# Householder steps on 65 rows and columns, and first-layer products in halves

## The chip, the cores and the metric

One core of one Trainium2 chip runs the whole kernel: a stack of four graph layers in float32. The metric is the device time of one execution in microseconds, the median of three runs. The engines are called PE (TensorE, matmuls; PEld is its weight loads), DVE (VectorE), ACT (ScalarE), POOL (GpSimd) and SP (SyncE, which issues DMAs).

## The reference

`x` is 128 x 64 x 256 (batch, nodes, features), `adj` is one 64 x 64 matrix for all. Every layer is `x = x + layer(relu(layernorm(x)))`. The layers, cut to what matters here:

```
# layer 0: graph convolution, two linear maps with batch norms
A_hat = (A + I) scaled on both sides by deg^-1/2
x1  = einsum('nm,bmd->bnd', A_hat, h).reshape(-1, 256)
h1  = relu(batchnorm(x1 @ W1.T + b1))          # 256 -> 512, statistics over all 8192 rows
out = batchnorm(h1 @ W2.T + b2)                # 512 -> 256, statistics over all 8192 rows
# layer 1: spectral layer
L_norm = d^-1/2 (diag(deg) - A) d^-1/2
_, U = eigh(L_norm)                            # 64 x 64, all eigenvectors
out = U @ (relu(U.T @ h @ W1 + b1) @ W2 + b2)  # over the nodes
# layer 2: two graph mixings, then LSTMs over windows of 1 to 4 nodes
# layer 3: attention over 512 edges, softmax by source node
```

The eigenvectors depend only on `adj`; layer 0 does not need them, layer 1 needs them from its first block on.

## The kernel before

The tokens (batch x node) are cut into 16 blocks of 512. `X[i]` holds block i in SBUF.

**Layer 0** (`hidden0`, `hidden_block`, `features0`). For each block: ReLU of the normalised block on ACT into `z`; the mixing with `BDH` (two copies of A_hat on a diagonal) on PE, 128 columns at a time, copied back to `z` by ACT; then four output groups of `W1`, each the sum of two products of 128 x 128 weights by 512 columns, `ps<-z,w` in the profile. A group's result stays in one PSUM bank, from which DVE takes statistics (`bn_stats`) and ACT a copy. Five banks are used in turn. When all blocks are through, `features0` takes the second linear map: per block four ReLUs on ACT, then two output groups, each the sum of four such products, which ACT copies out and squares for sums. That is 256 products of 512 columns. In the trace every float32 matmul shows as two records, each with a weight load.

**The eigenvectors** (class `Fast`). `tridiagonal` brings the 64 x 64 matrix `A` to tridiagonal form in 62 Householder steps, `householder(c)` for c from 63 to 2. Every row quantity is kept on all 64 partitions at once. One step: ACT sums the squares of row `x` (`f_ja`) and takes the root (`f_h_s`); DVE takes the reciprocal (`f_h_r`), corrects the root (`f_h_t`), multiplies by a sign half (`f_NB`), updates two elements of `x`, takes a reciprocal (`f_KAP`); ACT scales `x` to `uk`; DVE takes a dot product of `uA` and `uk` (`f_junk`), makes `v`, and from `uk`, `v` and a row `z` the next row `x` in two operations. Beside this, PE makes the outer products `uk v` and `v uk` (one row each), DVE adds them to `A`, PE multiplies a broadcast unit column and a broadcast column of `A` with `A` (`zp`, `yp`), ACT copies `zp` to `z`, and DVE makes `uA` of `z` and `yp`. A DMA on SP puts `x` into row c of `V`.

After the last step, `vectors` scales the matrix, turns the reflectors into one matrix (`reflectors`), finds the eigenvalues with two chains of polynomials on DVE (`values`), the eigenvectors of the tridiagonal matrix (`twisted`), the eigenvectors `U`, and a verdict on them (`f_k_bad`). All engines read the verdict and branch on it (L1617, L1618): where it is bad, another method runs. Layer 1 follows the branch.

**The order.** `Plan` writes the order of layer 0 and of the Householder steps by hand: each step has an engine (T for PE, S for ACT, V for DVE), a figure for how long it holds the engine and one for when its result is ready. `chain` places a Householder operation; before it, `fill` puts in layer-0 steps (`beside`) that end within a slack (0.6 us on T, 0.3 on S and V) of the time at which the chain operation could start. The instructions are issued in exactly this order up to the last Householder operation; layer-0 steps that found no place come out after `vectors`, and a scheduler merges them with the eigenproblem's instructions on each engine's queue. Each engine then works through its queue in order.

Engine calls go through a helper, so nearly all instructions show line L799; groups are told apart by tile names. `f_` is the tile prefix of class `Fast`, `fps` and `fvps` are its PSUM tiles.

Of the kernel before, what the change touches and what calls it, by code (L numbers as in the profile page):

```python
# [8 lines left out]
F32 = mybir.dt.float32  # L9
# [775 lines left out]
GRID = 64  # L785

# [126 lines left out]
class Fast:  # L913
# [31 lines left out]
    def sum(self, out, a, s, b, op0, op1=ALU.mult, name="junk"):  # L945

        w = a.shape[-1]
        j = self.t(f"{name}{a.shape[0]}", a.shape[0], 64)
        self.o.stt(j[:, 0:w], a, s, b, op0, op1, acc=out)
# [3 lines left out]
    def constants(self):  # L953
# [6 lines left out]
        self.P = t("P", 64, 1)  # L960
        iota(self.P[:], [[0, 1]], 0, 1)
# [21 lines left out]
        o.ts(self.low[:], self.J[:64, :], self.P[:], ALU.is_lt)  # L983
# [3 lines left out]
        o.copy(pi[:], self.P[:])  # L987
# [15 lines left out]
    def tridiagonal(self, S, made, plan):  # L1003
# [3 lines left out]
        A = self.A = t("A", 64, 64)  # L1007
        m = t("SR", 64, 64)
        NB, OA, KAP, V = t("NB", 64, 64), t("OA", 64, 64, 2), t("KAP", 64, 64), t("V", 64, 64)
        nc.vector.memset(OA[:], 1.0)  # L1010
        for x in (KAP, NB, V):
            nc.vector.memset(x[:], 0.0)
        s0, r, tt, q, c2 = (t("h_" + x, 64, 1) for x in "s0 r t q c2".split())
        ja = t("ja", 64, 64)
        bc = lambda c, n=64: c.to_broadcast([n, 64])
# [5 lines left out]

        d = go("T", lambda: keep("p", S, self.JR[:]), [made], 0.3, 0.5)
        d = go("V", lambda: o.copy(m[:], now["p"][:]), [d], 0.15, 0.28)
        d = go("T", lambda: keep("p", self.JR[:], m[:]), [d], 0.3, 0.5)
        rest = go("V", lambda: o.copy(A[:], now["p"][:]), [d], 0.15, 0.28)
        d = go("T", lambda: keep("p", bc(ident[:64, 63:64]), A[:]), [rest], 0.3, 0.5)

        def first():
            x = now["x"] = self.rows.tile([64, 65], F32, name="f_x", bufs=8)
            o.copy(x[:, 0:63], now["p"][:, 0:63])  # L1030

        def square(w):
            x = now["x"]
            self.act(ja[:, 0:w], x[:, 0:w], AF.Square, accum_out=x[:, w:w + 1])

        row = go("V", first, [d], 0.15, 0.28)
        h = go("S", lambda: square(63), [row], 0.34, 0.42)
        for c in range(63, 1, -1):
            row, h, rest = self.householder(c, now, go, row, h, rest, (s0, r, tt, q, c2), square)

    def householder(self, c, now, go, row, h, rest, scalars, square):

        o, nc, t = self.o, self.nc, self.t
        ident = self.k.ident
        A, NB, OA, KAP, V = self.A, t("NB", 64, 64), t("OA", 64, 64, 2), t("KAP", 64, 64), t("V", 64, 64)
        s0, r, tt, q, c2 = scalars
        bc = lambda a, n=64: a.to_broadcast([n, 64])
        x = lambda a, b: now["x"][:, a:b]
        nb = NB[:, c - 1:c]
        e, w = 0.001 * c, c - 1  # L1050

        def zy():
            now["zp"] = self.ps.tile([64, 64], F32, name="fps")
            nc.tensor.matmul(now["zp"][:, 0:c], bc(ident[0:c, c - 1:c], c), A[0:c, 0:c], start=True, stop=True)
            now["yp"] = self.ps.tile([64, 64], F32, name="fps")
            nc.tensor.matmul(now["yp"][:, 0:c], bc(A[0:c, c:c + 1], c), A[0:c, 0:c], start=True, stop=True)

        def row_z():
            now["z"] = self.rows.tile([64, 64], F32, name="f_z")
            self.act(now["z"][:, 0:c], now["zp"][:, 0:c], AF.Copy)  # L1060

        def row_uk():

            nc.sync.dma_start(V[c:c + 1, 0:c], now["x"][0:1, 0:c])
            now["uk"] = self.rows.tile([64, 64], F32, name="f_uk")
            self.act(now["uk"][:, 0:c], x(0, c), AF.Copy, scale=KAP[:, c:c + 1])

        def row_uA():
            now["uA"] = self.rows.tile([64, 64], F32, name="f_uA")
            o.stt(now["uA"][:, 0:c], now["z"][:, 0:c], nb, now["yp"][:, 0:c], ALU.mult, ALU.add)  # L1070

        def row_v():
            now["v"] = self.rows.tile([64, 64], F32, name="f_v")
            o.stt(now["v"][:, 0:c], x(0, c), c2[:], now["uA"][:, 0:c], ALU.mult, ALU.subtract)

        def outer():
            uk, v = now["uk"], now["v"]
            p = now["p"] = self.ps.tile([64, 64], F32, name="fps")
            nc.tensor.matmul(p[0:c, 0:c], uk[0:1, 0:c], v[0:1, 0:c], start=True, stop=False)
            nc.tensor.matmul(p[0:c, 0:c], v[0:1, 0:c], uk[0:1, 0:c], start=False, stop=True)  # L1080

        def row_x():
            now["x"] = self.rows.tile([64, 65], F32, name="f_x", bufs=8)
            o.stt(x(0, w), now["uk"][:, 0:w], now["v"][:, w:c], now["z"][:, 0:w], ALU.mult, ALU.add)


        z = go("T", zy, [rest], 0.34, 0.42)
        sq = go("S", lambda: self.act(s0[:], x(c, c + 1), AF.Sqrt), [h], 0.13, 0.23)
        oa = go("S", lambda: self.act(OA[:, c, 1:2], x(c - 1, c), AF.Copy), [row], 0.12, 0.22)
        zs = go("S", row_z, [z], 0.15, 0.26 + e)  # L1090
        sg = go("V", lambda: o.ts(q[:], x(c - 1, c), **halve(0)), [row])
        d = go("V", lambda: o.recip(r[:], s0[:]), [sq])
        d = go("V", lambda: o.stt(tt[:], r[:], x(c, c + 1), s0[:], ALU.mult, ALU.add), [d, h])
        b = go("V", lambda: o.mul(nb, q[:], tt[:]), [d, sg])
        d = go("V", lambda: o.stt(x(c - 1, c + 1), OA[:, c, :], nb, x(c - 1, c + 1), ALU.mult, ALU.add), [b, oa])
        d = go("V", lambda: o.recip(KAP[:, c:c + 1], x(c, c + 1)), [d])
        uk = go("S", row_uk, [d], 0.16, 0.32 + e)
        d = go("V", row_uA, [zs, b, z], 0.12 + e, 0.25 + e)
        d = go("V", lambda: self.sum(c2[:], now["uA"][:, 0:c], 0.5, now["uk"][:, 0:c], ALU.mult), [uk, d],
               0.2 + e, 0.28 + e)  # L1100
        v = go("V", row_v, [d], 0.15 + e, 0.26 + e)
        p = go("T", outer, [v], 0.25, 0.45)
        if c > 2:
            row = go("V", row_x, [v], 0.15 + e, 0.22 + e)
            row = go("V", lambda: o.stt(x(0, w), now["v"][:, 0:w], now["uk"][:, w:c], x(0, w), ALU.mult, ALU.add),
                     [row], 0.15 + e, 0.25 + e)
            h = go("S", lambda: square(w), [row], 0.28 + e, 0.36 + e)
        rest = go("V", lambda: o.add(A[0:c, 0:c], A[0:c, 0:c], now["p"][0:c, 0:c]), [p], 0.12 + e, 0.22 + e)
        return row, h, rest

    def reflectors(self):
# [8 lines left out]
        self.sum(kc[:], self.KAPs[:], 1.0, ident, ALU.mult)  # L1120
# [22 lines left out]
    def scale(self):  # L1143

        o, nc, t = self.o, self.nc, self.t
        NB, A = t("NB", 64, 64), self.A
        self.KAPs = t("KAP", 64, 64)
        DM, NE = t("DM", 64, 64), t("NE", 64, 64)
        o.mul(DM[:], A[:], self.k.ident[:64, :64])
        pe = self.mm((self.k.ident[:64, 1:2].to_broadcast([64, 64]), A[:]))  # L1150
# [223 lines left out]
    def verdict(self, U):  # L1374
# [32 lines left out]
        NB, OA = t("NB", 64, 64), t("OA", 64, 64, 2)  # L1407
# [36 lines left out]
P = 128  # L1444
# [1342 lines left out]
```

## Time and profile before

| what | us |
|---|---|
| median of 3 runs (2323.7 to 2329.91) | 2329.01 |
| span of the profiled execution | 2325.1 |
| first and last root of the Householder steps (`f_h_s`) | 12.1 and 268.3 |
| last 512-wide layer-0 product | 363.8 |
| verdict on the eigenvectors on PE (`f_k_bad`) | 364.35 |
| last 128-wide product after the branch, layer 1's start | from 370.16 |

The profiled execution's own time is its span, 2325.1 us, which lies inside the range of the runs; the median is 3.9 above it.

A group of the profile reads: line, engine, operation, output <- inputs by tile names, partitions x elements, how often, then busy time and mean duration in ns, then idle time of the engine ahead of it and what ended it. In the time-ordered view a row is start, duration, engine, line, operation, tiles, partitions x columns of the weights and elements, count, and in brackets the idle time of the engine before it. Rows are merged where one follows another, so a row's count matters. Ends of matmuls are modelled, so their durations overlap; distances between starts tell more.

### The profile page before, as it was taken

To read this page: it belongs to the slowest core of one execution; us is meant where nothing else is said; L and a number is where in the kernel's file an instruction comes from. 1 tells how busy PE (TensorE), PEld (TensorE's weight loads), DVE (VectorE), ACT (ScalarE), POOL (GpSimd) and SP (SyncE) were. 2 spreads that over 40 slices of the span, in tenths; PEclk is the share of its full clock that TensorE was granted. 3 is DMA by queue.
4 is the path that set the end of the run, shared out by engine and by line. 5 is a ranking of instruction groups with operands and counts; after the bars stand their busy time and mean duration, and the time that the engine had idled before them with its cause. 6 is when DMAs were issued, how large, how long until landed. Compare 5 with 4: busy or idle time off the path is not lost.

```text
span 2325.1 us, 32725 instructions
## 1 busy us (share of the span) xinstructions
PE 2283.6 (98%) x12169; PEld 1633.1 (70%) x12169; DVE 1629.3 (70%) x4054; ACT 1139.5 (49%) x2483; POOL 3.0 (0%) x26
## 2 busy tenths in 40 slices
PE   7999998999999999999999999999999999999999
PEld 4554445676777788888999998888885544554544
DVE  8887676888447777666767676559756686766667
ACT  5765865754436654433444444336435544444321
POOL 0000000000000000000000000000000000000000
PEclk9999999999999999999999999999999999999999
DMA  5000211230000000001000002000010000000001
GB/s 171 1 1 26 65 56 30 71 83 19 1 37 0 1 19 1 1 1 37 1 1 1 1 1 73 1 1 17 1 46 28 1 5 15 15 19 14 14 24 46
DMA packets 61065, 54.81 MB, mean 24 GB/s; under 512 B 15203, under 2 KB 58724, under 8 KB 60900
## 3 DMA queue, kind: packets, MB, share of 16 engines
q1 hardware_dynamic: 60900, 52.66, 7.4%
q8 instruction: 97, 1.59, 0.3%
q14 instruction: 68, 0.56, 0.1%
HBM read 35.86 MB, written 16.78 MB: 23 GB/s over the span
## 4 chain that ended last, share of the span: by engine, by line
PE 79%; DVE 3%; issue 1%; ACT 1%; DMA 0%; SPq 0%; ACTq 0%; DVEq 0%
PE ps L799 69%; PE acc L799 5%; PE pt L799 4%; PE pe L799 1%; PE y L799 1%; DVE aw L799 1%; DVE X L799 1%; DVE sm_m L799 0%; DVE XV L799 0%; ACT ls_g L799 0%; ACT h L799 0%; DVE ls_g L799 0%; ACT big L799 0%; DVE ls_t L799 0%; DVE sm_e L799 0%
## 5 line engine op out<-in xcount | busy, mean ns | idle before, releaser
L799 ACT ACTIVATE ls_g<-ls_g,ls_b 128x512 f32<-128x512 f32 (+4 forms) x472 | 243.1, 565 | 151.4 <-DVE ls_g L799 149.6
L799 ACT ACTIVATE ls_g<-ps,ls_b 128x256 f32<-128x256 f32 (+3 forms) x268 | 115.5, 470 | 330.9 <-PE ps L799 327.7
L799 PE MATMUL ps<-z,w 128*128 128x512 f32 x512 | 254.9, 621 | 0.9 <-ACT z L799 0.9
L799 PE MATMUL ps<-big,X 128*128 128x176 f32 (+3 forms) x848 | 212.7, 366 | 0.1
L799 DVE TENSOR_TENSOR ls_g<-ls_z,ps 128x512 f32<-128x512 f32 (+5 forms) x256 | 146.8, 579 | 91.9 <-PE ps L799 90.4
L799 DVE TENSOR_TENSOR aw<-at,ed_OST 128x1024 f32<-128x1024 f32 x128 | 149.9, 1219 | 83.0 <-PE ps L799 82.8
L799 PE MATMUL ps<-ls_tx,X 128*128 128x160 f32 (+2 forms) x960 | 206.8, 326 | 0.6 <-ACT ls_g L799 0.6
L799 PE MATMUL ps<-X,X 128*128 128x160 f32 (+1 forms) x896 | 199.1, 306 | 0.0
L799 PE MATMUL ps<-X,ls_w 128*128 128x256 f32 x640 | 190.5, 379 | 0.0
L799 PEld LDWEIGHTS ps<-ls_tx,X 128*128 128x128 f32 x960 | 161.8, 190 | 15.1 <-DVE X L799 4.8
L799 PEld LDWEIGHTS ps<-big,X 128*128 128x128 f32 x848 | 145.9, 190 | 29.7 <-issue 19.4
L799 DVE TENSOR_TENSOR X<-ls_g 128x1024 f32<-128x1024 f32 (+2 forms) x108 | 117.4, 1087 | 49.9 <-ACT ls_g L799 49.8
L799 ACT ACTIVATE r<-ps 128x512 f32<-128x512 f32 x256 | 131.6, 614 | 41.5 <-PE ps L799 41.4
L799 PEld LDWEIGHTS ps<-X,X 128*128 128x128 f32 x896 | 148.4, 190 | 0.0
L799 PE MATMUL ps<-X,ls_s 128*128 128x256 f32 x480 | 142.3, 379 | 0.0
L799 PEld LDWEIGHTS ps<-z,w 128*128 128x128 f32 x512 | 87.2, 190 | 69.0 <-issue 60.2
L799 PE MATMUL ps<-ls_tx,ls_s 128*128 128x256 f32 x464 | 134.8, 379 | 0.0
L799 PE MATMUL ps<-ed_S,Q 64*128 64x512 f32 x512 | 132.9, 618 | 1.4 <-DVE hT L799 0.7
L799 PE MATMUL ps<-ls_tx,ls_w 128*128 128x256 f32 x464 | 133.2, 380 | 0.0
L799 PEld LDWEIGHTS ps<-X,ls_w 128*128 128x128 f32 x640 | 121.4, 190 | 16.8 <-DVE X L799 0.3
L799 PE MATMUL ps<-big,ls_w 128*128 128x256 f32 x464 | 131.9, 379 | 0.7 <-ACT ls_z L799 0.7
L799 PE MATMUL ps<-aw,ed_ODT 128*64 128x512 f32 x512 | 117.3, 595 | 0.1
(545 smaller groups left out, 4019.0 us busy)
## 6 DMA issues: line engine op xcount, KB each, us to landing
X<-in_x_dram SPq DMA_DIRECT2D x32, 512.0 KB
xs<-X SPq DMA_DIRECT2D x16, 512.0 KB
X<-xs SPq DMA_DIRECT2D x16, 512.0 KB
out_dram<-X SPq DMA_DIRECT2D x31, 256.0 KB
X<-in_L_gnn_Wih_t_dram SPq DMA_DIRECT2D x4, 512.0 KB
ls_w<-in_L_gnn_Wih_t_dram SPq DMA_DIRECT2D x4, 512.0 KB
ls_w<-in_L_gnn_Whh_t_dram SPq DMA_DIRECT2D x4, 512.0 KB
w<-in_L_gnn_W_t_dram SPq DMA_DIRECT2D x2, 512.0 KB
```

Source lines behind the costliest of these rows:

```text
L799: i = method(*a, **kw)
```

## The change

The same Householder steps are computed with other shapes and in another grouping, and the layer-0 products are issued in halves.

- `A`, the rows and the per-step scalars have 65 partitions (`R = 65`) instead of 64 or c. The products `zp` and `yp` take all 65 rows of `A` and a column broadcast to 65; for `yp` the column is first multiplied by a mask (`xc`, on DVE), so that rows beyond c count for nothing. `zp` and `yp` are two plan steps instead of one.
- The outer products take `x0` (row `x` with all partitions but the first set to zero, made by ACT) and `v`, 65 rows and 65 columns each, instead of one row; they are not scaled by KAP. The update of `A` on DVE does that scaling.
- `NB` is no longer made in the step: ACT scales `OA` and a copy `zq` of `zp` by the sign half `q`, and DVE uses `TT` (the corrected root) where it used `NB`. ACT makes a second, unscaled copy `z`. `scale` makes `NB` for all steps at once.
- The dot product takes `uA` and `x` instead of `uA` and `uk`; `v` is `uk` times the dot product less `uA`.
- Every 512-column product of layer 0 becomes two of 256 columns, and every mixing of four 128-column products becomes two steps of two.

```diff
+R = 65
...
-        def zy():
-            now["zp"] = self.ps.tile([64, 64], F32, name="fps")
-            nc.tensor.matmul(now["zp"][:, 0:c], bc(ident[0:c, c - 1:c], c), A[0:c, 0:c], start=True, stop=True)
-            now["yp"] = self.ps.tile([64, 64], F32, name="fps")
-            nc.tensor.matmul(now["yp"][:, 0:c], bc(A[0:c, c:c + 1], c), A[0:c, 0:c], start=True, stop=True)
+        def product(name, column):
+            now[name] = self.ps.tile([R, 64], F32, name="fps")
+            nc.tensor.matmul(now[name][:, 0:c], self.wide(column), A[:, 0:c], start=True, stop=True)
+
+        def copied(name, scale):
+            now[name] = self.rows.tile([R, 64], F32, name="f_" + name)
+            self.act(now[name][:, 0:c], now["zp"][:, 0:c], AF.Copy, scale=scale)
...
         def outer():
-            uk, v = now["uk"], now["v"]
-            p = now["p"] = self.ps.tile([64, 64], F32, name="fps")
-            nc.tensor.matmul(p[0:c, 0:c], uk[0:1, 0:c], v[0:1, 0:c], start=True, stop=False)
-            nc.tensor.matmul(p[0:c, 0:c], v[0:1, 0:c], uk[0:1, 0:c], start=False, stop=True)
+            p = now["p"] = self.ps.tile([R, 64], F32, name="fps")
+            nc.tensor.matmul(p[:, 0:c], x0[:, 0:R], v[:, 0:c], start=True, stop=False)
+            nc.tensor.matmul(p[:, 0:c], v[:, 0:R], x0[:, 0:c], start=False, stop=True)
...
-        z = go("T", zy, [rest], 0.34, 0.42)
-        oa = go("S", lambda: self.act(OA[:, c, 1:2], x(c - 1, c), AF.Copy), [row], 0.12, 0.22)
-        zs = go("S", row_z, [z], 0.15, 0.26 + e)
-        sg = go("V", lambda: o.ts(q[:], x(c - 1, c), **halve(0)), [row])
-        d = go("V", lambda: o.recip(r[:], s0[:]), [sq])
-        d = go("V", lambda: o.stt(tt[:], r[:], x(c, c + 1), s0[:], ALU.mult, ALU.add), [d, h])
-        b = go("V", lambda: o.mul(nb, q[:], tt[:]), [d, sg])
-        d = go("V", lambda: o.stt(x(c - 1, c + 1), OA[:, c, :], nb, x(c - 1, c + 1), ALU.mult, ALU.add), [b, oa])
-        d = go("V", lambda: o.recip(KAP[:, c:c + 1], x(c, c + 1)), [d])
-        uk = go("S", row_uk, [d], 0.16, 0.32 + e)
-        d = go("V", row_uA, [zs, b, z], 0.12 + e, 0.25 + e)
-        d = go("V", lambda: self.sum(c2[:], now["uA"][:, 0:c], 0.5, now["uk"][:, 0:c], ALU.mult), [uk, d], ...)
-        v = go("V", row_v, [d], 0.15 + e, 0.26 + e)
-        p = go("T", outer, [v], 0.25, 0.45)
+        sg = go("V", lambda: o.ts(q, x(c - 1, c), **halve(0)), [row], 0.09, 0.25)
+        m = go("V", lambda: o.mul(xc[:], A[:, c:c + 1], self.MK[:, c:c + 1]), [rest], 0.09, 0.25)
+        z = go("T", lambda: product("zp", ident[0:R, c - 1:c]), [rest], 0.13, 0.38)
+        y = go("T", lambda: product("yp", xc[:]), [m], 0.13, 0.38)
+        oa = go("S", lambda: self.act(OA[:, c, 1:2], x(c - 1, c), AF.Copy, scale=q), [row, sg], 0.13, 0.25)
+        zs = go("S", lambda: copied("zq", q), [z, sg], 0.15, 0.27 + e)
+        d = go("V", lambda: o.recip(r[:], s0[:]), [sq], 0.09, 0.25)
+        d = go("V", lambda: o.stt(tt, r[:], x(c, c + 1), s0[:], ALU.mult, ALU.add), [d, h], 0.09, 0.25)
+        zc = go("S", lambda: copied("z", 1.0), [z], 0.15, 0.27 + e)
+        uA = go("V", row_uA, [d, zs, y], 0.12 + e, 0.25 + e)
+        d = go("V", lambda: o.stt(x(c - 1, c + 1), OA[:, c, :], tt, x(c - 1, c + 1), ALU.mult, ALU.add), [d, oa], ...)
+        u = go("S", lambda: self.act(x0[:, 0:c], x(0, c), AF.Copy, scale=self.E0[:]), [d], 0.16, 0.3 + e)
+        k = go("V", lambda: o.recip(kap, x(c, c + 1)), [d], 0.09, 0.25)
+        uk = go("S", row_uk, [k], 0.16, 0.32 + e)
+        d = go("V", lambda: self.sum(dd[:], now["uA"][:, 0:c], 0.5, x(0, c), ALU.mult), [uA, d], ...)
+        d = go("V", lambda: o.stt(v[:, 0:c], now["uk"][:, 0:c], dd[:], now["uA"][:, 0:c], ALU.mult, ALU.subtract), [d, uk], ...)
+        p = go("T", outer, [d, u], 0.25, 0.47)
...
-        rest = go("V", lambda: o.add(A[0:c, 0:c], A[0:c, 0:c], now["p"][0:c, 0:c]), [p], 0.12 + e, 0.22 + e)
+        rest = go("V", lambda: o.stt(A[0:c, 0:c], now["p"][0:c, 0:c], KAP[0:c, c:c + 1], A[0:c, 0:c], ALU.mult, ALU.add), ...)
...
-            x = beside("T", lambda hc=hc: product(hc, 0), mixed, 0.86, 0.9, bank)
-            x = beside("T", lambda hc=hc: product(hc, 1), [x], 0.86, 1.0)
+            x = beside("T", lambda hc=hc: product(hc, 0, 0), mixed, 0.43, 0.43, bank)
+            for k, kc in ((0, 1), (1, 0), (1, 1)):
+                x = beside("T", lambda hc=hc, k=k, kc=kc: product(hc, k, kc), [x], 0.43, 0.6 if k and kc else 0.43)
...
-                for kc in range(4):
-                    x = beside("T", lambda oc=oc, kc=kc, f=product: f(oc, kc), [z[kc]] + ([x] if x else []), 0.86, 1.0, ...)
+                for k in range(2):
+                    for kc in range(4):
+                        x = beside("T", lambda oc=oc, k=k, kc=kc, f=product: f(oc, k, kc), [z[kc]] + ([x] if x else []), 0.43, 0.6, ...)
```

## The prediction

> **What bounds the kernel now.** I read the page first, then busy time by stage, then the instructions in order of time inside the stage that the diff touches, TensorE (PE) apart from the rest. The page alone says little: PE is busy everywhere.
>
> ```profile
> PE 2283.6 (98%) x12169; PEld 1633.1 (70%) x12169; DVE 1629.3 (70%) x4054; ACT 1139.5 (49%) x2483; POOL 3.0 (0%) x26
> ```
>
> Only the first layer changes. By stage, with the columns PE, weight load, DVE, ACT, POOL, clock, DMA share:
>
> ```profile
> 12.00:270.00 258.00, 248.22 (x1152) 129.37 (x1152) 194.54 (x1003) 176.50 (x604) 0.00 (x0) 0.99 0.14 41
> 270.00:365.00 95.00, 91.87 (x312) 40.98 (x310) 71.25 (x344) 58.29 (x147) 0.00 (x0) 1.00 0.18 53
> ```
>
> 12 to 270 is the 62 Householder steps, with layer-0 work in between; 270 to 365 is the rest of the eigenproblem, again with layer-0 products in between. To know whether PE is full in fact, I count starts, not busy shares. PE around step c=43:
>
> ```profile
> 103.98 0.27 PE L799 MATMUL fps<-f_v,f_uk 1*44 1x44 f32 x2
> 104.26 1.13 PE L799 MATMUL ps<-z,w 128*128 128x512 f32 x2
> 105.32 0.31 PE L799 MATMUL fps<-f_A,ident 43*64 43x43 f32 x2
> 105.67 0.70 PE L799 MATMUL ps<-z,w 128*128 128x512 f32 x1
> ```
>
> A 512-wide product (two records) runs at 0.857 us inside a stream (the loads below: 0.43 per record). Here it takes 105.32-104.26 = 1.06, so 0.20 is lost around it. The outer product pair holds PE for 0.28, the z,y pair for 0.35. Why 0.20: the loads show it.
>
> ```profile
> 101.74 0.19 PEld L799 LDWEIGHTS ps<-z,w 128*128 128x128 f32 x1 [0.24 <-issue]
> 103.98 0.15 PEld L799 LDWEIGHTS fps<-f_v,f_uk 1*44 1x44 f32 x2 [0.76 <-issue]
> ```
>
> A load for the same shape of array starts 0.24 after the last one ended, under the running product; one for a small matrix starts after 0.76, when PE has emptied, and the first 128x128 load afterwards is bare as well. Between two full-size shapes nothing is lost: 8 records in 0.89, then straight on.
>
> ```profile
> 111.10 1.05 PE L799 MATMUL ps<-BDH,z 128*128 128x128 f32 x8
> 111.99 1.02 PE L799 MATMUL ps<-z,w 128*128 128x512 f32 x2
> ```
>
> PE's sum for the 62 steps of before, with counts from the issue order: 175 products x 0.857 = 150; 128 mixings and 28 warm-ups x 0.223 = 34.8; chain products 62 x (0.28+0.35) = 39; 117 visits to them x 0.20 = 23. Together 247 of 258: PE is the bound, and a quarter of it is the chain's.
>
> The dependent chain is close behind. DVE in a little disturbed step (c=29):
>
> ```profile
> 164.41 0.21 DVE L799 SCALAR_TENSOR_TENSOR f_h_t<-f_h_r,f_x,f_h_s 64x1 f32<-64x1 f32 x1
> 164.65 0.15 DVE L799 TENSOR_TENSOR f_NB<-f_h_q,f_h_t 64x1 f32<-64x1 f32 x1
> 164.91 0.21 DVE L799 SCALAR_TENSOR_TENSOR f_x<-f_OA,f_NB,f_x 64x2 f32<-64x2 f32 x1
> 165.72 0.18 DVE L799 SCALAR_TENSOR_TENSOR f_junk<-f_uA,f_uk 64x29 f32<-64x29 f32 x1
> 165.94 0.24 DVE L799 SCALAR_TENSOR_TENSOR f_v<-f_x,f_h_c,f_uA 64x29 f32<-64x29 f32 x1
> 167.59 0.21 DVE L799 SCALAR_TENSOR_TENSOR f_h_t<-f_h_r,f_x,f_h_s 64x1 f32<-64x1 f32 x1
> ```
>
> From h_t to h_t 3.18 us, against a mean of 258/62 = 4.16.
>
> **The change, part by part.**
>
> *65 rows and columns.* Row: 0.20 per visit. The Trainium skill's TensorEngine Tiling (Array Packing), Key Properties, says that changing the tiling mode drains TensorE, and its modes end at 64; so 65x65 would run in the full array's mode and the drain would go. No product between 65 and 127 is in this trace; what the trace has is the BDH line above. The same page's When to Use Tiling speaks against the change: dimensions up to 64 belong in small tiles. It is about several tiles at once, and here every product stands alone; by it 65 rows would gain nothing, and 117 x 0.20 = 23 us would stay. The load of 64 columns is 0.058 per record:
>
> ```profile
> 283.96 0.54 PEld L799 LDWEIGHTS fvps<-f_SG,f_I2T 128*64 128x64 f32 x8
> ```
>
> (0.54-0.13)/7. A step has 8 records: 62 x 8 x 0.058 = 29. After each visit the next 128x128 load (0.107 in the BDH stream) outlasts the last small product by 0.05: 117 visits (as many in the new issue order) x 0.05 = 6. Chain on PE: 35 instead of 62, 27 saved. Bounds: 0 (no drain removed, full-width loads of 0.107: 53 + 23, even 14 worse) to 29. I take 27, nearest to the BDH row.
>
> *256-wide products.* 256 products become 512, with twice the loads. A load (0.19) must hide under half a product. The LSTM stage streams 256 columns:
>
> ```profile
> 700.40 2.56 PEld L799 LDWEIGHTS ps<-ls_tx,X 128*128 128x128 f32 x12
> ```
>
> (2.56-0.19)/11 = 0.215 per record, twice that is the 0.43 of a 512-wide record. Cost 0 in the stream; bound 256 x 0.02 = 5. Gain: a chain product waits behind at most 0.43, not 0.86.
>
> *Out of the chain.* The NB multiplication goes (164.65 to 164.91: 0.26), and the dot product no longer waits for uk, so v follows uk directly (165.72 to 165.94: 0.22). The scaling by KAP moves into the update of A. 3.18-0.48 = 2.70. Added to it: in the new DVE order uA stands directly ahead of x in all 62 steps (before: behind KAP), so x, KAP, both ACT copies and v queue behind uA, and uA waits for y. At the 0.16 that it issues in: 2.86. The second loop is v, outer, A, mask (xc, new, 0.15 as NB; 0.25 with its latency), y: v to A at best 0.63, xc at 0.95, up to two half products (0.86), y at about 1.9 after v; uA's other input is there at about 2.0. Level, so uA costs little while PE is punctual. Layer-0 work in the queues (a bn_stats holds DVE 0.68, a ReLU ACT 0.59) adds 0.2 to 0.3. I take 3.1 for a step that PE does not set.
>
> *ACT and DVE.* ACT gets x0 (like f_uk, 0.20 apart) and a second copy of z (0.10): 62 x 0.3 = 19 us under PE's products. DVE loses NB and gains xc. Counted per step, ACT has 163 us and DVE 156 in some 222: cover holds on the mean. The 62 DMAs of V stay; SP is not waited for. Extra memsets are on POOL or ahead of the first step, two small operations in the scaling: under 0.5.
>
> *The sum.* New order: by the last step 150 products' worth are issued, not 175. PE: 150 x 0.857 + 34.8 + 35 = 198. Taking for each step the longer of its own PE work and 3.1 gives 220; the same sum for before, with 3.4, gives 256 where 258 were measured, so +2: 222. Steps start at 12, end at 234 (before 270). Then the eigenproblem: from 268.3 (last f_h_s) to its verdict at 364.35 it took 96 with 81 products inside; now 76.5 are: 96-4.5 x 0.857 = 92, verdict at 326. What is late next: 29.5 products are left, 25.3 us of PE alone (ACT's 5.3 per block, 4 ReLUs 0.70 apart, 2 copies 0.58 and 2 squares 0.67, is under PE's 6.9). Last product at about 352 instead of 364.4.
>
> ```profile
> 364.35 0.27 PE L799 MATMUL fps<-f_k_bad,ones 64*64 64x1 f32 x2
> 364.66 0.15 DVE L799 CAST f_k_badi<-fps 64x1 int32<-64x1 f32 x1 [0.98 <-PE fps L799]
> 372.03 0.81 ACT L799 ACTIVATE big<-big,bn_sh,bn_sc 128x512 f32<-128x512 f32 x1 [1.41 <-DVE bn_sh L799]
> ```
>
> The branch and the statistics to 372 stay; the flag is ready early (0.5). Gain 12.5+0.5 = 13: 2325.1-13 = 2312, and the median stands 3.9 above this execution's span: **2316 us**. 0.1 us per step is 2 to 4 us.
>
> **Rivals.** *PE stays full:* the saved 27 come whole: 2302. For it: PE's 95% now, finer steps. Against: 25 of the 62 steps have under 3.2 us of PE work. *The gain is swallowed:* drain not removed, or steps of 3.7: 12+229 = 241+117 = 358, gain 6 or less, 2323 to 2333. For it: DVE and ACT go to 85% of a shorter stage. *Slower:* uA ahead of x: if y is late by 0.9 in each step (A behind bn_stats, y behind three half products), the chain waits on DVE's queue; steps of 4.0 put the last at 260, the end at 377, 2342. It decides from 3.82 (no gain) and 3.94 (0.3% slower) per step.
>
> **How the numbers follow.** Main case 0.48 (2309 to 2322), PE full 0.20, swallowed 0.20, slower 0.12. Measurement tells 0.3%, 7 us, from nothing: faster 0.68, same 0.19, slower 0.13. Range 2300 to 2332; the main case's own is 2309 to 2322.
>
> **What would show it.** Small products entered at 0.43 after the last record, loads with no 0.76; z,w at 0.215 per record; last f_h_s at 230 to 240; the verdict 20 to 30 us before the last layer-0 product. Wrong if the 0.76 stays, if DVE idles before uA on PE, or if steps stay at 4.

## The result, and the profile after

The changed kernel takes 2335.75 us (median of 6 runs, 2333.93 to 2336.03), the kernel before in the same comparison 2328.65. The ratio is 1.0031, with an interval of 1.0019 to 1.0042: 0.3% slower, where 2316 was forecast. The profiled execution's span is 2332.1, 7.0 above that of before (2325.1).

The stages of the changed kernel, in the columns of the windows shown of before (PE, weight load, DVE, ACT, POOL, clock, DMA share, GB/s). The cuts lie at the last root of the steps (254.5) and at the verdict (348.7):

```profile
12.00:255.00 243.00, 221.27 (x1393) 185.79 (x1394) 189.71 (x998) 187.44 (x683) 0.00 (x0) 0.98 0.13 39
255.00:349.00 94.00, 91.07 (x467) 70.01 (x466) 72.44 (x350) 63.44 (x156) 0.00 (x0) 1.00 0.20 57
349.00:375.00 26.00, 25.61 (x118) 22.21 (x118) 0.13 (x1) 14.14 (x36) 0.00 (x0) 1.00 0.14 43
```

The steps end 13.8 us earlier than before (268.3 to 254.5), the verdict comes 15.7 us earlier, and then PE sets the pace for another 25.5 us with 29 products that found no place earlier (DVE is busy for 0.13 of these 26 us, ACT for 14). The last product starts at 374.2; before it was 363.8. The rest of the kernel is the same: from `bn_sh`, the last operation of the batch norm, to the end it is 1953.2 us before and 1953.1 after.

Loads and products around one step, in order of time:

```profile
102.58 0.25 PEld L800 LDWEIGHTS fps<-f_v,f_x 65*65 65x65 f32 x2
102.75 0.20 PEld L800 LDWEIGHTS fps<-f_x,f_v 65*65 65x65 f32 x2
103.09 0.30 PEld L800 LDWEIGHTS ps<-z,w 128*128 128x128 f32 x2
103.43 0.33 PEld L800 LDWEIGHTS fps<-f_A,ident 65*65 65x65 f32 x2
...
101.79 1.06 PE L800 MATMUL ps<-BDH,z 128*128 128x128 f32 x8
...
103.09 0.70 PE L800 MATMUL ps<-z,w 128*128 128x256 f32 x2
103.62 0.26 PE L800 MATMUL fps<-f_A,ident 65*65 65x41 f32 x2
103.83 2.84 PE L800 MATMUL ps<-z,w 128*128 128x256 f32 x12
```

No load here waits in idle time for PE to empty; the 0.76 of before is gone, and the small loads at 102.58 start under the mixings (101.79, 1.06 long). The load at 103.43 starts 0.19 ahead of its product (103.62). In the run that puts the same kernel back on 64 rows, the same pair of instructions starts at one time, the load after 0.33 idle:

```profile
103.77 0.19 PEld L800 LDWEIGHTS fps<-f_A,ident 64*64 64x64 f32 x2 [0.33 <-DVE f_h_r L800]
...
103.77 0.31 PE L800 MATMUL fps<-f_A,ident 64*64 64x42 f32 x2
```

So the drain is gone as forecast. What PE waits for in the steps instead (waits between 12 and 255: who waits, for whom, us in all, how often, longest), cut to the lines that matter, first of the kernel before, between 12 and 270:

```profile
...
DVE f_A L799 <- PE fps L799: 21.6, 41, 1.1
ACT f_z L799 <- PE fps L799: 21.0, 40, 1.0
```

then of the changed kernel:

```profile
PEld fps L800 <- DVE f_v L800: 20.5, 24, 2.7
...
DVE f_v L800 <- ACT f_uk L800: 14.2, 41, 0.5
PE fps L800 <- DVE f_v L800: 13.9, 15, 2.5
...
DVE f_uA L800 <- ACT f_zq L800: 8.5, 15, 1.4
...
DVE f_A L800 <- PE fps L800: 6.1, 10, 2.5
...
DVE f_uA L800 <- PE fps L800: 2.2, 2, 1.9
```

Before, DVE and ACT waited for PE; after, PE waits for `v`, the end of the dependent chain. By the prediction's own sum PE has 198 us of work in the steps; they last 242.4, so it stands idle for some 44 us. This is an estimate: the view above has no PE product running for 21.7 of the 243 us, but the ends of products in it are modelled.

The end of the stage, in order of time:

```profile
348.67 0.27 PE L800 MATMUL fps<-f_k_bad,ones 64*64 64x1 f32 x2
...
375.43 0.19 DVE L800 TENSOR_REDUCE bn_a<-sums 128x2 f32<-128x32 f32 x1 [26.30 <-ACT big L800]
...
379.19 1.52 ACT L800 ACTIVATE big<-big,bn_sh,bn_sc 128x512 f32<-128x512 f32 x2 [1.41 <-DVE bn_sh L800]
```

DVE waits 26.3 us for the last products. From the last product to `bn_sh` it is 4.8 us (before 8.0): the branch on the verdict now lies under the products, which gives 3.2 back.

### The profile page after: what moved, and what is told of

Same layout as the page of the kernel before. It is cut to its first block, busy times and chain, and to the rows that moved or that the text cites. A ratio compares the mean times of both kernels' runs of the same rounds, so it can differ in the third digit from the quotient of the medians.

```text
span 2332.1 us, 33840 instructions
## 1 busy us (share of the span) xinstructions
PE 2279.0 (98%) x12681; PEld 1738.2 (75%) x12681; DVE 1626.6 (70%) x4057; ACT 1171.6 (50%) x2607; POOL 3.3 (0%) x30
## 4 chain that ended last, share of the span: by engine, by line
PE 79%; DVE 3%; issue 1%; ACT 1%; DMA 0%; ACTq 0%; DVEq 0%
PE ps L800 68%; PE acc L800 5%; PE pt L800 4%; PE pe L800 1%; PE y L800 1%; DVE aw L800 1%; DVE X L800 1%; DVE sm_m L800 0%; DVE XV L800 0%; ACT ls_g L800 0%; DMA X<-in_L_gnn_Wih_t_dram 0%; DVE ls_g L800 0%; DMA ls_w<-in_L_gnn_Wih_t_dram 0%; ACT big L800 0%; ACT h L800 0%
## 5 line engine op out<-in xcount | busy, mean ns | idle before, releaser
L800 PE MATMUL ps<-z,w 128*128 128x256 f32 x1024 | 259.8, 397 | 2.4 <-ACT z L800 1.9
L800 PEld LDWEIGHTS ps<-z,w 128*128 128x128 f32 x1024 | 187.5, 194 | 29.5 <-ACT z L800 5.7
L800 ACT ACTIVATE big<-ps 128x512 f32<-128x512 f32 x96 | 69.2, 751 | 95.9 <-PE ps L800 93.2
```

The source lines that it names most:

```text
L800: i = method(*a, **kw)
```

## The experiments

The theories. **A:** the stage ends at PE's work plus its idle time, and PE is idle because too few first-layer products lie between the steps; a shorter chain alone brings nothing. **B:** `uA` ahead of `x` makes the steps long. **Halves:** the loss comes from the halved products and not from the new steps. Others (C, H, L, Q) are told where they arise. In the text "by the last root" means first-layer products, counted as whole 512-wide ones, started by the time of the last `f_h_s` of the steps. The runs stand in several comparisons, each with the kernel before beside it, whose median was 2327.10 to 2329.32; so a difference of up to some 2 us between runs of different comparisons is not told from none.

### uA late

```diff
-        uA = go("V", row_uA, [d, zs, y], 0.12 + e, 0.25 + e)
+        tq = d
...
         k = go("V", lambda: o.recip(kap, x(c, c + 1)), [d], 0.09, 0.25)
+        uA = go("V", row_uA, [tq, zs, y], 0.12 + e, 0.25 + e)
```

> The row uA is issued behind the reciprocal that makes kap instead of ahead of x; nothing else is changed. Theory B (the long step comes from uA standing in front of x on VectorE): a step loses at least 0.33 us, the shortest stretch from tt to uA, so the last step ends near 234 us instead of 254.5, TensorE idles some 20 us less in the steps, and the kernel takes 2312 to 2320 us. Theory A (TensorE stands idle because too few first-layer products lie between the steps; the stage ends at TensorE's work plus its idle time, whatever the chain does): the steps do end earlier, by 15 to 30 us, but the products that do not fit between shorter steps stand behind the last one, TensorE's idle time does not fall, and the kernel takes 2336 us or more, up to 2365.

Measured: 2385.35 us, ratio 1.0245 (1.023 to 1.026). Theory B's time does not come. A has its sign right, but the loss is larger than its range, and the steps do not end 15 to 30 us earlier: the last root is at 251.6, 2.9 earlier, with 96 products done by then instead of 146. 84 are left after the verdict, and the last starts at 426.6. One thing clouds the reading of the step: the granted clock was low in it, while in the products left over it was full (columns as above).

```profile
110.00:160.00 50.00, 40.84 (x212) 33.41 (x213) 38.28 (x202) 30.56 (x126) 0.00 (x0) 0.73 0.01 1
160.00:210.00 50.00, 39.19 (x202) 32.31 (x201) 33.66 (x185) 30.12 (x130) 0.00 (x0) 0.69 0.01 1
...
354.00:427.00 73.00, 73.00 (x339) 64.01 (x338) 0.15 (x1) 53.36 (x124) 0.00 (x0) 1.00 0.23 66
```

How many products stand ahead of the last step is written in the issue order, so the low clock did not lower their number. The run shows what too few products cost (72 us behind the verdict, at full clock), but not what the place of `uA` is worth to the step; that needed the runs further down.

### The two parts alone

The kernel before with the first-layer part of the diff, and the changed kernel without it:

```diff
-            x = beside("T", lambda hc=hc: product(hc, 0), mixed, 0.86, 0.9, bank)
-            x = beside("T", lambda hc=hc: product(hc, 1), [x], 0.86, 1.0)
+            x = beside("T", lambda hc=hc: product(hc, 0, 0), mixed, 0.43, 0.43, bank)
+            for k, kc in ((0, 1), (1, 0), (1, 1)):
+                x = beside("T", lambda hc=hc, k=k, kc=kc: product(hc, k, kc), [x], 0.43, 0.6 if k and kc else 0.43)
```

> The kernel before with the first layer's 256-wide products and half mixings alone; the Householder steps are the old ones on 64 rows. Theory A (the loss sits in the new steps, which leave TensorE unfilled): within 0.3% of before, 2322 to 2335 us, with every further switch between sizes at 0.2 us as the only possible loss. The rival (the halves themselves are the loss, through more switches or more idle between them): 2334 to 2342 us, and the new steps on their own would be a gain.

Measured: 2333.20 us, ratio 1.0021 (1.0012 to 1.0030), inside theory A's range at its upper end, but 4.6 us above before and not the same as it.

> The changed kernel with the first layer's products 512 wide and its mixings in one piece again; the Householder steps are the new ones on 65 rows. Theory A: the new steps still leave TensorE idle for some 40 us or more, since the ScalarE copies are the same and the pieces to fill with are coarser: 2334 to 2345 us. The rival (the halves are the loss): 2312 to 2320 us.

Measured: 2321.97 us, ratio 0.9975 (0.9967 to 0.9983). This is a miss for theory A, and 2 us above the range of its rival: the new steps alone make the kernel 6.7 us faster, and the halves on top of them cost 13.8. (The profiled execution took 2325.9, so its rows are some 4 us late.) The step is the same 3.95 us as with halves (3.98), but 156 products are done by the last root instead of 146, and 16 instead of 29 are left at the verdict. So what decides is how many products lie beside steps of one length, as theory A has it, but it is the halves that lower the number, which A had put down to the new steps alone.

### The drain put back

```diff
-R = 65
+R = 64
```

> The changed kernel with R = 64, so that the chain's products lie on 64 rows and columns again, with the same operations and the same order otherwise. Prediction: a drain of 0.20 us comes back at some 117 visits, 23 us of TensorE's time, and since the small products are on the path both ways the kernel takes up to 27 us longer, 2355 to 2363 us. Theory A: part of the drain falls in time in which TensorE is idle anyway (44 us in the steps), so 5 to 20 us: 2341 to 2356 us. If the drain is hidden altogether: 2334 to 2338 us.

Measured: 2350.38 us, ratio 1.0097, 14.6 above the changed kernel. Theory A's range holds. The order and the products by the last root are the same (146); each step is 0.21 longer (4.19).

### A longer look ahead

Why do halves lower the number of products laid? `fill` tries the first 12 pieces of an engine's queue. A block has 20 PE pieces in halves and 10 in whole ones.

```diff
-            for x in self.queue[engine][:12]:
+            for x in self.queue[engine][:24]:
```

> The changed kernel with one number different: the plan looks for a piece that fits among the next 24 in an engine's queue instead of the next 12. Theory L (the halves lose because twelve half pieces reach only half as far ahead, so that the plan more often finds nothing that may start): most of the 13.8 us between the changed kernel and the one with the new steps alone come back, 2322 to 2329 us, and by 120 us about 64 first-layer products have been done instead of 56. Rival (a half product costs TensorE more than half of a whole one, through the second weight load or more waits in front of loads): the look-ahead changes nothing, 2333 to 2338 us.

Measured: 2325.40 us, ratio 0.9988 (0.9981 to 0.9995). One number in the plan brings 10.4 of the 13.8 us back; by 120 us 64 products are done (56 in the changed kernel, 64 with the new steps alone), by the last root 158.

> The old steps with the halves, and a look-ahead of 24 pieces. Theory L: the 4.6 us that the halves cost by themselves come back, 2326 to 2331 us. Rival (the halves cost TensorE more by themselves): 2332 to 2336 us.

Measured: 2329.08 us, ratio 1.0003 (0.9995 to 1.0010): the old steps with halves are level with before. Both lie in theory L's ranges. But a longer look ahead also helps the new steps with whole products (next runs, there with a larger slack), so that what came back need not all be the halves' own loss: at equal reach, 24 half pieces against 12 whole ones, 3.4 us remain between 2325.40 and 2321.97.

### More laid beside the steps

The run with `uA` late again, now with a plan that can fill it, and the new steps with whole products, filled (two runs in one cut, the comments added):

```diff
-            plan = Plan(dict(T=0.6, S=0.3, V=0.3), 5)
+            plan = Plan(dict(T=0.6, S=0.5, V=0.4), 5)     # uA late, look-ahead 24
+            plan = Plan(dict(T=0.6, S=0.4, V=0.3), 5)     # whole products, look-ahead 20
```

> The row uA behind kap as in the first run, with a look-ahead of 24 and slacks of 0.5 us for ScalarE and 0.4 us for VectorE in place of 0.3, so that the plan may lay more beside the same short chain. Theory A (the end is TensorE's work plus its idle time; the chain alone decides nothing): the 50 us of the first run come back and more, since the chain of the first run was no longer than that of the changed kernel: 2312 to 2325 us. Rival (uA late is itself what made 2385: a wait of uA, or of v for it, in the chain): 2350 us or more whatever is laid beside it.

Measured: 2318.71 us, ratio 0.9961 (0.9946 to 0.9975). The same chain as in the 2385 us kernel, 66.6 us faster: 169 products by the last root instead of 96, and a clock of 0.97 in the steps.

> The new steps with whole 512-wide products, a look-ahead of 20 and a slack of 0.4 us for ScalarE. Theory A: of the 27 us of drain that the new steps take from TensorE, the new steps alone gave 6.7 and left the rest as idle time; with the gaps filled the idle time in the steps falls by some 10 us, last product and verdict come both near 357 us, and the kernel takes 2311 to 2319 us, below both kernels. Rival (TensorE's gaps are the chain's own, 3.9 us a step, and nothing can be laid into them): 2320 to 2326 us, as with the new steps alone.

Measured: 2312.06 us, ratio 0.9931 (0.9918 to 0.9944), the fastest kernel of the study, below before and below the changed kernel. 173 products are done by the last root at 254.3, the place of the changed kernel's (254.5); last product (348.8) and verdict (349.8) come together.

```profile
12.00:255.00 243.00, 232.23 (x1153) 134.43 (x1154) 189.63 (x1001) 200.38 (x721) 0.00 (x0) 1.00 0.15 43
255.00:350.00 95.00, 91.88 (x311) 40.93 (x309) 72.20 (x349) 61.60 (x155) 0.00 (x0) 1.00 0.19 56
```

Against the first line of the changed kernel PE has 11 us more busy time in the same 243 us, ACT 13 more, and DVE the same: 27 more products beside the steps did not lengthen them. Look-ahead and slack were changed together here, and no run parts them.

### Controls on the fill

The kernel before with the look-ahead of 20 and S=0.4; the filled steps on `R = 64`; the changed kernel, halves and all, with the same fill; and, in the changed kernel as it is, a third ACT copy in each step:

```diff
         zc = go("S", lambda: copied("z", 1.0), [z], 0.15, 0.27 + e)
+        go("S", lambda: self.act(self.ja[:, 0:c], now["z"][:, 0:c], AF.Copy), [zc], 0.15, 0.27 + e)
```

> The control: the kernel before with the look-ahead of 20 and the slack of 0.4 us for ScalarE that brought the new steps with whole products to 2312 us. If the gain of that run is the new steps' (their freed 27 us of TensorE, made use of): before stays within 0.3% of itself, 2322 to 2334 us, since TensorE was already full in its steps. Rival (the gain was the plan's alone): 2310 to 2316 us, and the new steps are worth nothing.

Measured: 2328.69 us, ratio 0.9997 (0.9988 to 1.0006). The fill does nothing for the old steps (171 products by the last root with and without); the gain at 2312 needs the new ones.

> The new steps with whole products, filled as before (look-ahead 20, slack 0.4 us), but on 64 rows and columns. The prediction's price of the drain is 0.20 us a visit, some 120 visits to the end of the steps and some 25 us in all. Theory A (an idle TensorE hides the drain, a filled one pays it): more of it is paid than the 14.6 us of the changed kernel, 18 to 27 us over the same kernel on 65 rows, 2330 to 2339 us. Rival (it is the chain's latency that pays, at so many visits a step, whether TensorE is filled or not): 14 to 15 us as there, 2326 to 2327 us.

Measured: 2333.09 us, ratio 1.0021 (1.0015 to 1.0028), 21.0 above the same kernel on 65 rows. With the steps filled more of the drain is paid than the 14.6 above, as theory A has it.

> The changed kernel, halves and all, with the look-ahead of 20 and the slack of 0.4 us. If halves cost nothing once the plan looks far enough: 2310 to 2315 us, as with whole products. If a half still costs (four loads for two, more waits in front of loads, a plan that fits them worse): 2316 to 2324 us.

Measured: 2325.31 us, ratio 0.9984 (0.9977 to 0.9990). Just above both ranges: 13.2 above the filled steps with whole products. With the same number of pieces to choose from, halves thus cost as much as before (13.8). 20 half pieces reach only as far as 10 whole ones; a run of halves at equal reach and with the larger slack is missing.

> The changed kernel with one more ScalarE copy in each of the 62 steps (the row z once more, into a row that nothing reads). Theory C (the two copies that the new steps add to ScalarE leave the first layer's inputs no room, and so starve TensorE): as much again as two copies are said to have cost, half of TensorE's 33 us more idle time for one copy, 10 to 17 us: 2345 to 2353 us. Rival (ScalarE has room; what lacks is pieces that the plan may lay): within 4 us of the changed kernel, 2332 to 2340 us.

Measured: 2340.78 us, ratio 1.0047 (1.0031 to 1.0063), 5.0 above the changed kernel (3.7 by the ratios): far from theory C, and 0.8 above the rival's range. A copy in each step is not free (last root and last product both 3.0 later), but the room of ACT does not explain 44 us of idle PE.

### Which halves, and on what

Three runs on the filled steps (2312.06 us). In the first the plan is unchanged, and a piece of `W1` issues two 256-wide matmuls instead of one of 512; in the others the halves of one matrix (with `W1` those of the mixings too) are pieces of the plan, as in the diff above. All have a look-ahead of 20 pieces, so that in the last two it reaches less far where pieces are halves.

```diff
-            self.mm(now["p", hc][:], W1[:, kc, hc * P:(hc + 1) * P], now["z"][:, 2 + kc, :], kc == 0, kc == 1)
+            s = slice(D * k, D * k + D)
+            for kc in range(2):
+                self.mm(now["p", hc][:, s], W1[:, kc, hc * P:(hc + 1) * P], now["z"][:, 2 + kc, s], kc == 0, kc == 1)
```

> The new steps filled as in the 2312 us kernel, pieces and plan the same, but a piece of the W1 products issues two 256-wide matmuls (its two halves of the sum over the inputs) where it issued one of 512; mixings and W2 products are whole. If a half costs TensorE by itself (a second load, a wait in front of it): 128 products that take up to 0.05 us more, 2315 to 2320 us. If only the plan lays halves worse: 2310 to 2314 us.

Measured: 2313.67 us, ratio 0.9936 (0.9922 to 0.9950), 1.6 above, no more than comparisons tell apart. On PE itself 128 halved products cost next to nothing.

> The filled steps with the mixings and the W1 products in halves as pieces of the plan, the W2 products whole. If the plan lays halves worse, and this in the steps (at 120 us the changed kernel had 65 products where whole ones had 72): 6 to 12 of the 13 us between the two filled kernels, 2318 to 2324 us. If the loss is W2's, in the eigenproblem: 2311 to 2315 us.

Measured: 2315.04 us, ratio 0.9947 (0.9930 to 0.9963), 3.0 above, a miss for the expectation that the loss is mainly here.

> The filled steps with the W2 products alone in halves, mixings and W1 whole. If the loss is W1's in the steps: 2312 to 2316 us, the 3 us being what the eigenproblem showed, where halves let 26 visits of small products in where whole products had 19 to 22 in the same 75 us. If the loss is W2's: 2318 to 2325 us.

Measured: 2320.33 us, ratio 0.9960 (0.9945 to 0.9976), 8.3 above: of the two, `W2` costs more. By 260 us 173.8 products are done where whole ones have 178.5; and in the eigenproblem, where a scheduler and not the plan merges the products in, fewer get through. Products on PE between 262 and 347, two records for a whole one and four for a halved one; first whole:

```profile
L800 PE MATMUL ps<-z,w 128*128 128x512 f32 x147 | 70.2, 611 | 0.0
```

then halved:

```profile
L800 PE MATMUL ps<-z,w 128*128 128x256 f32 x283 | 71.0, 398 | 0.0
```

147/2 = 73.5 against 283/4 = 70.75, 2.75 products or 2.4 us at 0.857. The same shows between kernels: in the 90 us after the last root 0.87 to 0.89 products a microsecond where `W2` is whole, 0.83 to 0.85 where it is halved (the run with `uA` late left out, which still has `W1` to do there). Why is open. It is tempting to put it down to small products that break in more often where pieces are small: between 270 and 345 there are 19 to 22 such visits in before, in the new steps alone and in the filled steps, and 25 to 27 in the changed kernel, its filled form and the old steps with halves. But the filled steps with `W2` halved have 23, the changed kernel with a third copy has 21, and whole products on 64 rows, filled, have 26, so the count of visits does not go with the rate.

### Nothing beside the steps

The same edit in three kernels: before, changed, and changed with `uA` late.

```diff
-        while True:
+        while until >= 1e9:
             best = None
```

> The kernel before with nothing laid beside the 62 steps: the plan holds all of the first layer back until they are over (all is still computed, later). Only the step is read from it, not the time of the kernel, which must be some 80 us longer or more. By the prediction's hops the bare old chain is 3.18 us a step, the last step near 209 us; if the hops were mis-sized 3.8 us or more, near 250.

Measured: median step 3.15 us (mean 3.29 with the first six, which share DVE with the setting up of the first layer), last root 219.0. The median is the prediction's 3.18 but for 0.03; the last root comes 10 us later than expected, the first one being at 18.6.

> The changed kernel with nothing laid beside the steps. By the prediction's hops: 2.86 us a step, last step near 190 us. Theory Q (what is laid between lengthens the chain through the order in the queues): 2.8 to 3.2 us, against 3.9 to 4.1 with products between. Theory H (the chain itself is the 3.9 us, through uA ahead of x or a hop that was left out): 3.7 to 4.0 us, last step near 250.

Measured: median step 3.06 us (mean 3.16), last root 211.8. Theory Q holds: bare, the new step is 3.06, 0.2 above the prediction's 2.86; with products beside it, 3.9 to 4.1 on the mean.

> As the run before with uA behind kap. By the prediction uA stands 0.16 us in the way: 2.70 us a step. If uA waits for y or zq there and holds x up (the prediction's slower rival): 0.33 us or more shorter than with uA early. If nothing waits on it: within 0.05 us of it.

Measured: median step 2.87 us (mean 3.01), last root 202.8. `uA` ahead of `x` costs 0.15 (means) to 0.19 (medians), as the prediction's 0.16 had it, and not theory B's 0.33. These three are single executions, read for the step alone.

DVE in one bare new step:

```profile
130.76 0.21 DVE L800 SCALAR_TENSOR_TENSOR f_TT<-f_h_r,f_x,f_h_s 65x1 f32<-65x1 f32 x1
131.19 0.24 DVE L800 SCALAR_TENSOR_TENSOR f_uA<-f_zq,f_TT,fps 65x30 f32<-65x30 f32 x1 [0.22 <-ACT f_zq L800]
...
132.16 0.25 DVE L800 SCALAR_TENSOR_TENSOR f_v<-f_uk,f_h_d,f_uA 65x30 f32<-65x30 f32 x1 [0.31 <-ACT f_uk L800]
...
133.79 0.21 DVE L800 SCALAR_TENSOR_TENSOR f_TT<-f_h_r,f_x,f_h_s 65x1 f32<-65x1 f32 x1
```

and in a step of the changed kernel:

```profile
167.87 0.21 DVE L800 SCALAR_TENSOR_TENSOR f_TT<-f_h_r,f_x,f_h_s 65x1 f32<-65x1 f32 x1
168.00 0.69 DVE L800 BATCH_NORM_STATS2 st<-ps 128x6 f32<-128x512 f32 x1
168.61 0.22 DVE L800 SCALAR_TENSOR_TENSOR f_uA<-f_zq,f_TT,fps 65x25 f32<-65x25 f32 x1
...
170.42 0.69 DVE L800 BATCH_NORM_STATS2 st<-ps 128x6 f32<-128x512 f32 x1
171.03 0.21 DVE L800 SCALAR_TENSOR_TENSOR f_A<-fps,f_KAP,f_A 25x25 f32<-25x25 f32 x1
...
171.54 0.21 DVE L800 SCALAR_TENSOR_TENSOR f_TT<-f_h_r,f_x,f_h_s 65x1 f32<-65x1 f32 x1
```

Bare: 3.03 from `f_TT` to `f_TT`, `uA` 0.43 behind it. With the first layer: 3.67, `uA` 0.74 behind, for a `bn_stats` stands between; a second one stands ahead of the update of `A`. A `bn_stats` stands between `f_TT` and `x` in 25 of the 62 steps. The means over steps 9 to 60, from start to start in the trace:

| hop | bare | changed | more |
|---|---|---|---|
| `f_TT` to `x` (over `uA`) | 0.60 | 0.90 | 0.30 |
| root to reciprocal (ACT to DVE) | 0.24 | 0.44 | 0.20 |
| `v` to next `x` | 0.28 | 0.42 | 0.14 |
| other seven hops of this loop | 1.90 | 2.14 | 0.24 |
| whole loop over the root | 3.02 | 3.90 | 0.88 |
| `yp` to `uA` (PE to DVE) | 0.50 | 0.84 | 0.34 |
| `v` to `A` (over PE) | 0.98 | 1.27 | 0.29 |
| `xc` to `yp` (DVE to PE) | 0.30 | 0.46 | 0.16 |

The extra 0.88 is no single wait: it is spread over the queues of all three engines.

The planner in the kernel's code shows where it comes from. The program's own figures, added up by its own `Plan`, put the last chain operation of the changed kernel at 248.9 (147 products laid ahead of it), and at 194.1 with nothing laid: 54.8 us for 62 steps, again 0.88 a step. With all three slacks at 0 it lays 8 products and ends at 194.4. So the first layer's work stands in the chain's way because the slack lets it: a piece may end up to 0.6 us (PE) or 0.3 us (ACT, DVE) behind the time at which the chain operation could have started. This is the plan's arithmetic and not a measurement; no run had a smaller slack. The same arithmetic shows that the number laid does not grow evenly with the look-ahead: halves at a slack of 0.4 get 170.5 with 20 pieces and 156 with 40, whole products at 0.3 get 154 with 12, 143 with 20 and 153 with 24.

### All in one table

| kernel | us | step | products by last root | last product | verdict, on DVE |
|---|---|---|---|---|---|
| before | 2328.65 | 4.20 | 171 | 363.8 | 364.7 |
| before, filled | 2328.69 | 4.22 | 171 | 364.7 | 365.5 |
| old steps, halves | 2333.20 | 4.16 | 162 | 371.9 | 359.6 |
| old steps, halves, look-ahead 24 | 2329.08 | 4.23 | 172 | 367.1 | 363.9 |
| changed | 2335.75 | 3.98 | 146 | 374.2 | 349.0 |
| changed, R = 64 | 2350.38 | 4.19 | 146 | 389.4 | 364.2 |
| changed, uA late | 2385.35 | 3.93 | 96 | 426.6 | 354.3 |
| changed, third copy | 2340.78 | 4.02 | 148 | 377.2 | 353.3 |
| changed, look-ahead 24 | 2325.40 | 3.90 | 158 | 359.8 | 344.9 |
| changed, filled | 2325.31 | 4.10 | 168 | 363.1 | 356.5 |
| uA late, filled | 2318.71 | 4.02 | 169 | 357.3 | 350.6 |
| new steps, whole products | 2321.97 | 3.95 | 156 | 364.0 | 350.7 |
| the same, filled | 2312.06 | 3.97 | 173 | 348.8 | 349.8 |
| the same, filled, R = 64 | 2333.09 | 4.31 | 173 | 369.9 | 370.9 |
| the same, filled, halves in pairs | 2313.67 | 3.99 | 173 | 350.2 | 351.2 |
| the same, filled, `W1` halved | 2315.04 | 4.02 | 170 | 353.8 | 354.7 |
| the same, filled, `W2` halved | 2320.33 | 4.03 | 172 | 357.3 | 353.2 |

`us` is the median of the runs, the rest is of the profiled execution; `step` is the mean, and the last two columns are starts.

The time goes with the later of the last two columns: `bn_sh` follows it by 5 to 8 us, and from there to the end these executions take 1952 to 1955.3. On 65 rows with a first layer beside it the step lies between 3.90 and 4.10, with 96 products laid (at the lower clock told above) or with 173.

## Why the prediction was wrong, by its steps

The forecast was 2316, within 2300 to 2332, with 0.68 on faster; it came out 0.3% slower, outside the range.

**Where the 20 us are.** The forecast made the sum 2312 for a span; the span is 2332.1. The last root was put at 234 and came at 254.5: 20.5. The eigenproblem was put at 92 and took 94.2: 2.2. The products left, 25.3, took 25.5. The flag was to give 0.5, and the hidden branch gave 3.2: 2.7 back. Together 20.2 of the 20.1. The size of the work left over and of the stage behind the steps was right; the length of the steps was not.

**The step that failed** is the 3.1 in the sum: "Taking for each step the longer of its own PE work and 3.1 gives 220". The 3.1 was a bare chain of 2.86 and "adds 0.2 to 0.3" for layer-0 work in the queues. Measured, the bare chain is 3.02 to 3.06, and what the first layer adds is 0.88: on each of three engines a chain operation waits out a piece of the first layer's work that the plan has put ahead of it. A step with products beside it takes 3.9, not 3.1. That a bare step comes out near 3.1 is chance, since 3.1 was meant for a step with products. Of the 0.8 us by which the 3.1 was short, some 0.2 are the bare chain's and some 0.6 the surcharge's, which was read off the length of single operations (a `bn_stats`, a ReLU) and not off the plan, whose slack allows more. The calibration on before did not show it: there PE's own work per step was so large that the longer of two came near the measured 258, with a surcharge of only 2. The rest of the sum stands up: the prediction itself puts the break-even at steps of 3.82 and 0.3% slower at 3.94, and with 3.9 to 3.98 the kernel is 0.3% slower. PE's 198 us were not measured by themselves; with the 146 products that had started by the last root, instead of 150, they would be 3 less.

**PE is the bound before:** no run speaks against it. A plan that looks further lays no more in the old steps (171 and 171, 2328.69 us), and DVE and ACT wait for PE there.

**The drain:** the mechanism is right, as the loads and the two runs on 64 rows show. 27 us were taken as the price; 21.0 are paid where PE is full, 14.6 in the changed kernel, as theory A has it: part of it there falls into time in which PE is idle anyway. Of the two readings of the Trainium skill's TensorEngine Tiling (Array Packing) the one from Key Properties held (a change of mode drains); by When to Use Tiling nothing would have been gained.

**Halves, "Cost 0 in the stream":** so they nearly are, on PE (1.6 us for half of them). In the kernel they cost 4.6 us on the old steps and 13.8 on the new ones. The prediction read from the issue order that 150 products instead of 175 come by the last step, and put it into the sum, but did not ask why. The run with a longer look-ahead answers: with 24 pieces instead of 12, 158 come and 10.4 us return. That 12 half pieces reach half as far explains it, but is not the whole account, since with the filled plan halves cost 13.2 again. A share sits in `W2`, 8.3 us with the filled plan, partly in the eigenproblem; why is open.

**The chain, 3.18 to 2.86:** bare it went from 3.15 to 3.06 (2.86 was forecast). `uA` ahead of `x` was put at 0.16 and costs 0.15 to 0.19. What was taken out gave 0.28 (3.15 to 2.87), not 0.48: between the bare old steps and the bare new ones with `uA` late, the corrected root to `x` falls by 0.19 and `uk` to `v` by 0.14.

**ACT under cover:** not free. A third copy costs 5.0 us (3.7 by the ratios); two copies may by this have cost 7 to 10, an estimate that no run tested.

**The rivals.** The slower one had the sign and the step (4.0), but not the mechanism: that its number came near is luck. It had DVE waiting for `y` ahead of `uA`, and this is 2.2 us in 2 of the 62 steps; on ACT's `zq` it waits 8.5 us, 0.14 a step. `uA` moved away made 2385, and with both filled it is level with `uA` early or a little shorter (4.02 against 4.10 a step). "PE stays full" at 2302 would have needed the fill; the filled steps reach 2312. "The gain is swallowed" named longer steps and busier queues, and came nearest to what happened; its steps of 3.7 and its 2323 to 2333 us fell short.

## What to carry to other kernels

Where two streams share in-order queues, don't size the chain from the lengths of its own operations: measure it bare, take the step with the other stream beside it from the trace, and treat the difference as a cost that stays when the chain gets shorter. Where a planner wrote the order, ask it first how long it makes the chain with the other stream and without. Work taken off the bound engine is a gain only where something is laid into the time that comes free; so when an issue order shows less work laid than before, find out why before costing anything else. A list scheduler's look-ahead is counted in pieces: after cutting the pieces in two, count again what it lays.

## What the runs showed of the hardware

The granted TensorE clock does not follow PE's share of busy time. In the run with `uA` late it fell to 0.69 to 0.80 between 110 and 252 us, with PE busy some 80% of the time. In the bare new steps, with PE busy for less than half, it stayed at 1.00:

```profile
20.00:212.00 192.00, 81.45 (x485) 64.53 (x486) 145.17 (x861) 103.89 (x497) 0.00 (x0) 1.00 0.08 23
```

In the steps of the changed kernel it was 0.98, in those of the filled ones with whole products 1.00. The means of the late run are mixtures: in finer windows the clock is either half or full, in stretches that are multiples of 3.41 us.

```profile
140.52:157.58 17.06, 14.37 (x54) 11.49 (x54) 11.26 (x57) 8.89 (x38) 0.00 (x0) 0.50 0.00 0
157.58:164.41 6.83, 5.36 (x46) 4.81 (x44) 4.65 (x28) 5.34 (x22) 0.00 (x0) 1.00 0.01 1
```

The Trainium skill's TensorE: Matmul & The Clock Gate (Part 1) has the clock halved after idle windows of about 3.4 us. The half clock and the length of the stretches agree with it. The idle window does not, if it means a window without work: the longest wait of PE or its weight loads between 110 and 252 in the late run is 1.7 us. In the bare steps, at full clock, it is 3.3, still shorter than the window. What sets the clock in these steps stays open.
